# Second softmax product moved between V's first tiles, and the score products in another order

## The chip, the cores and the metric

The kernel runs on one core of one Trainium2 chip. The core has five engines with queues of their own: TensorE (PE in the profile, with its weight loads listed as PEld), VectorE (DVE), ScalarE (ACT), GpSimd (POOL) and SyncE (SP, which here only issues DMAs). The metric is the device time of one launch in microseconds, as the median of several runs.

## The reference

For each of 16 batches there are 100 rows of hidden states `x` (640 wide) and a context of 722 rows (384 wide), of which the first 718 (`enc`) are keys and values and the last 4 (`ca`) are tokens. With 8 heads of 80:

```
query = x @ Wq ; keyt = enc @ Wk ; valt = enc @ Wv
hs = mha(query, keyt, valt)                  # 100 queries, 718 keys
ca_q1 = einsum('btc,th->bch', ca, Wq_ca)[:, indices]
ca_hs1 = mha(ca_q1, x, x)                    # 100 queries, 100 keys
ca_hs2 = mha(ca_hs1 @ Wq, ca @ Wk_ca, ca @ Wv_ca)   # 4 keys
out = (hs + ca_hs2) @ Wout + b_out + x
```

`mha` scales the scores by 80 to the power -0.5, takes a softmax over the keys and multiplies by the values. All is float32.

## The kernel before

Everything is one loop over the 16 batches; each engine's instructions run in the order in which the program issues them, and the order was written out by hand. Waits between engines are semaphores that follow from tiles: an instruction that writes a buffer waits until the last reader of what was in it is done.

**The products of a batch.** The 718 keys stand in six chunks of up to 120 (`KC`), two to a group, so three key groups g = 0, 1, 2. The scores of a group (`scores`, matmuls at L688) come in two kinds. The *heads* hold 64 of the 80 columns of each head: weights of 64 rows by 64 or 56 columns, four such tiles of the array side by side. The *others* hold the remaining 16 columns of all heads: weights of 32 rows by 120 columns, again four side by side. Each float32 product is two matmul records in the profile, so the heads of a group are 64 records and the others 16. Heads and others add up in the same banks. I write H0, H1, H2 and O0, O1, O2 for them. Before, the order is H0, O0, O1, H1, H2, O2.

Scores leave PSUM by ScalarE's copies into `st` (L719 for group 1, one for each of four banks, L725 for groups 0 and 2, one for each of two pairs of banks). VectorE takes a running maximum over the three groups (`most`: L1449, then `larger`, L1440), a chain of transposes and reductions (`Maximum`, L760 to L790) spreads it, and later the maximum is subtracted and exponentiated (L1428, L1436). At the end of the batch `r_ps` (L1579) and `a_ps` (L1597) are the products with V; ScalarE copies `a_ps` out into `hsT` (L1110, `keep`).

**The tokens' attention** (`Second`) runs one batch ahead in parts. `products` writes `y_ps` for the next batch (L836), `copy` copies it to `y` (ScalarE, L857), and `softmax2` multiplies the exponentials `e1` of the present batch with `y` into `z_ps` (L898, 64 small matmuls of 32 or 4 columns) and divides on VectorE (L907, L909). Since `y` has one buffer, `copy` for the next batch must follow `softmax2` of this one. `scores2` and `softmax3` go on with the quotient `z`.

**V and K.** `Values` makes V of this batch and `Keys` makes K of the next from sums of blocks, following lists of 15 products each (`V_PLAN`, `K_PLAN`). A product goes to one of the banks A to E; after each product the bank is copied (ScalarE) or added (VectorE) to its places (`Blocks.go`, L416 and L418). `vv.go(n)` and `kk.go(n)` issue n products; `both(n)` issues n of V, then n of K. The first three products of either list go to A, B and D. A V product is four records of 320 columns over the full array, a K product four of 240.

**PSUM.** It has eight banks: two pairs (`ps2`), two of `psk` and two of `ps1`. Groups 0 and 2 of the scores take both pairs, group 1 the four single banks. `v_psA` and `v_psB` take the pairs behind group 2 (the first V product, A, waits for the first of group 2's two copies, the second, B, for the second copy). `k_psA` and `k_psB` take `psk`. `r_ps`, `a_ps`, `z_ps`, `y_ps`, the two halves of `v_psD` and `k_psD` take turns on the two `ps1` banks: the fourth bank of group 1 is the one of `a_ps`, and `k_psD` takes the bank of the first half of `v_psD`.

The order before, from the first score on:

```
st.append(scores(b, 0, tiles)); ...; st.append(scores(b, 1, tiles)); larger(1)
st.append(scores(b, 2, tiles))
now.softmax2(); second.products(); second.copy()
seen = larger(2); ...; top.go(3); both(3)
now.scores2(); top.go(1); both(2); ...
```

Of the kernel before, what the change touches and what calls it, by code (L numbers as in the profile page):

```python
# [19 lines left out]
HC = H // P  # L20
# [127 lines left out]
def kernel(  # L148
# [41 lines left out]
    def pair(name):  # L190
        tile = ps2.tile([P, 2, 512], F32, tag="ps2", name=name)
        return tile
# [21 lines left out]
    def scores_tile(name):  # L214
        return main.tile([P, 2, ROWS], F32, tag="st", name=name, bufs=NP)
# [183 lines left out]
    class Blocks:  # L399


        def __init__(self, plan):
            self.opened, self.begun = {}, set()
            self.plan = iter(enumerate(plan))
            self.ends = {bank: k for k, (bank, _, _) in enumerate(plan)}
# [264 lines left out]
        )  # L670


    def scores(b, g, tiles):

        qp, qz = tiles
        name = f"s_ps_{b}_{g}"
        if g == 1:
            s_ps = [f(f"{name}_{r}") for r, f in enumerate((psumk, psumk, psum1, psum1))]
        else:
            pairs = [pair(f"{name}_{i}") for i in range(2)]  # L680
            s_ps = [pairs[r // 2][:, r % 2] for r in range(RG)]
        n = KN
        opened = set()

        def product(a, c, rows, keys, bank, lo, rhs, last):
            u, j = KC[2 * g + a]
            first = [k for k in (0, 64) if keys.start <= k < keys.stop and (bank, k) not in opened]
            nc.tensor.matmul(  # L688
                s_ps[bank][keys, 256 * a + lo : 256 * a + lo + rhs.shape[-1]],
                kT[rows, c, u, j * KN + keys.start : j * KN + keys.stop],  # L690
                rhs,
                start=bool(first),
                stop=last,
                skip_group_check=True,
            )
            opened.update((bank, k) for k in first)

        def heads(last):
            for a in range(2):
                for c in range(HC - 1):  # L700
                    for e in range(2):
                        at = 4 * e + c
                        rows = slice(64 * e, 64 * e + 64)
                        rhs = qp[rows, c // 2, c % 2, (b % 2) * S : (b % 2 + 1) * S]
                        for keys in (slice(0, 64), slice(64, n)):
                            product(a, c, rows, keys, at // 2, at % 2 * S, rhs, last)

        def others(last):
            for a in range(2):
                for r in range(RG):  # L710
                    rows = slice(32 * r, 32 * r + 32)
                    product(a, HC - 1, rows, slice(0, n), r, 0, qz[rows, 0, b % 2], last)

        for k, part in enumerate((others, heads) if g == 1 else (heads, others)):
            part(k == 1)
        st = scores_tile(f"st_{b}_{g}")[:n]
        if g == 1:
            for r in range(RG):
                nc.scalar.copy(  # L719
                    st[:, :, 2 * r * S : 2 * (r + 1) * S],  # L720
                    s_ps[r][:n].rearrange("p (a q) -> p a q", a=2)[:, :, : 2 * S],
                )
        else:
            for i in range(2):
                nc.scalar.copy(  # L725
                    st[:, :, 4 * i * S : 4 * (i + 1) * S].rearrange(
                        "p a (r q) -> p r a q", r=2
                    ),
                    pairs[i][:n].rearrange("p r (a q) -> p r a q", a=2)[:, :, :, : 2 * S],
                )  # L730
        return st

    def wait_for(ins, other):

# [80 lines left out]
    class Second:  # L815
# [77 lines left out]
        def softmax2(self):  # L893
            b = self.b
            z_ps = (psum1 if b + 1 < B else psumk)(f"z_ps_{b}")
            for h in range(NH):
                for lo, hi in QZ:
                    nc.tensor.matmul(  # L898
                        z_ps[lo:hi, h * (HT + 1) : (h + 1) * (HT + 1)],
                        e1[:S, h * S + lo : h * S + hi],  # L900
                        self.y[:, h, :],
                        start=True,
                        stop=True,
                    )
            z_v = z_ps[:S, : NH * (HT + 1)].rearrange("p (h k) -> p h k", h=NH)
            rz = small.tile([S, NH], F32, tag="rz", name=f"rz_{b}")
            nc.vector.reciprocal(rz.unsqueeze(2), z_v[:, :, HT:])  # L907
            z = small.tile([S, NH, HT], F32, tag="z", name=f"z_{b}")
            nc.vector.tensor_tensor(  # L909
                z, z_v[:, :, :HT], rz.unsqueeze(2).to_broadcast([S, NH, HT]), ALU.mult  # L910
            )
            self.z = z
# [497 lines left out]
    for b in range(B):  # L1410
# [27 lines left out]
        def larger(i):  # L1438
            for u in range(2):
                most_now = nc.vector.tensor_tensor(  # L1440
                    most[:KN], most[:KN], st[i][:, u], ALU.max
                )
            return most_now

        st.append(scores(b, 0, tiles))
        waiting = late
        if late:
            now.exponentials1()
        nc.vector.tensor_tensor(most[:KN], st[0][:, 0], st[0][:, 1], ALU.max)  # L1449
        st.append(scores(b, 1, tiles))  # L1450
        larger(1)
        if b == 0:
            now.exponentials1()
        st.append(scores(b, 2, tiles))

        vv = Values(b, e_in, V_PLAN if b + 1 < B else END_PLAN)
        if b + 1 < B:
            kk = Keys(b + 1, enc)
        now.softmax2()
        if b + 1 < B:  # L1460
            second.products()
            second.copy()
        seen = larger(2)
        top = Maximum(most, f"{b}", True)

        if b + 1 < B:

            def both(n):
                vv.go(n)
                kk.go(n)  # L1470

            if waiting:
                wait_for(enc_sums(enc, LATE_SUMS), seen)
            if waiting:
                second.scores1(tokens=range(T - 1))
            else:
                second.scores1(seen)
            store(seen)
            if last:
                last.load(seen)  # L1480
            if b == B - 2:
                again()
            if b + 2 < B:
                m_next = load_m(b + 2, seen)
            if b == 1:
                load_outputs(nc.sync.dma_start, wout_sb, wout)
            top.go(3)
            both(3)
            now.scores2()
            top.go(1)  # L1490
            both(2)
            top.go()
            both(2)
            now.softmax3()
            if waiting:
                second.scores1(tokens=range(T - 1, T))
            if b + 2 < B:
                keys(m_next)
            both(1)
            now.spread2()  # L1500
            vv.go(2)
            kk.go(1)
            subtract(0)
            exponential(0)
            vv.go(1)
            less = subtract(1)
            if last:
                last.place(less)
                if last.b in PAIRED:
                    last.row_sums()  # L1510
                last.add_bias()
            if b == B - 2:
                mine.load(seen)
            now.values2()
            if b == B - 2:
                mine.add_bias()
            vv.go(1)
            kk.go(2)
            exponential(1)
            vv.go(1)  # L1520
            kk.go(2)
            both(1)
            both(1)
            if b == 1:
                nc.gpsimd.dma_start(out=bias, in_=bout[0].partition_broadcast(P))
            second_next, enc_next = loads()
            subtract(2)
            exponential(2)
            last_keys(b + 1, enc, b in (6, 7))
            if b + 2 < B:  # L1530
                enc_next = load_rest(b + 2, enc_next)
        else:
            last.place()
            mine.load(seen)
            top.go(3)
            vv.go(3)
            top.go(1)
            now.scores2()
            last.project_few(len(OC) - 2)
            last.project((0,), True, put=False)  # L1540
            top.go()
            now.softmax3()
            vv.go(1)
            now.spread2()
            vv.go(1)
            less = subtract(0)
            exponential(0)
            wait_for(subtract(2, nc.gpsimd), less)
            subtract(1, nc.gpsimd)
            mine.add_bias()  # L1550
            now.values2()
            vv.go(5)
            exponential(2)
            vv.go(1)
            exponential(1)
            vv.go(4)
            last.put()
# [109 lines left out]
```

## Time and profile before

| | us |
|---|---|
| median of 3 runs | 914.13 (914.01 to 916.65) |
| profiled execution, its device time | 915.1 |
| its span, first to last instruction | 913.4 |
| busy: PE, DVE, POOL, ACT | 907.1, 668.5, 619.4, 375.2 |

In the profile a row of the timeline gives start, length from the first start to the last end, engine, line, operation, tile out and in, shape and count, and in brackets the engine's idle time before it with what ended that. Matmuls overlap, so the time from the start of one row to the start of the next tells how long PE was taken. A row of a group gives busy time and the mean of one in ns, then the engine's idle time before these instructions. The granted TensorE clock is 1.0 in the whole span.

### The profile page before, as it was taken

What the parts mean: (1) busy time and instruction counts of PE and PEld (TensorE: products, weight loads), DVE (VectorE), ACT (ScalarE), POOL (GpSimd) and SP (SyncE); (2) the same over time, 40 slices, a digit from 0 to 9 for tenths busy, and PEclk for the clock granted to TensorE, in tenths of its full rate; (3) what the DMA queues carried; (4) which work ended last, traced back from release to release, by engine and by line L of the source; (5) the groups of instructions that cost most, each with busy time, mean ns of one, the idle gap of its engine ahead of it and who ended that gap; (6) DMA issues with size and microseconds to landing.
All of it is one profiled execution on the core that took longest, in us unless ns stands there. A gap on an engine that the chain in (4) does not pass through costs nothing.

```text
span 913.4 us, 26025 instructions
## 1 busy us (share of the span) xinstructions
PE 907.1 (99%) x11127; PEld 758.2 (83%) x11127; DVE 668.5 (73%) x1121; ACT 375.2 (41%) x649; POOL 619.4 (68%) x653
## 2 busy tenths in 40 slices
PE   9999999999999999999999999999999999999998
PEld 7988889787887879878788888988888888887865
DVE  4899795979649796676957769588782888828773
ACT  1354534444334453443434434344541445424451
POOL 9664786677847788476674756755796567955635
PEclk9999999999999999999999999999999999999999
DMA  8604351141302303140221402304140151401313
GB/s 275 231 13 134 61 126 37 25 124 40 103 12 71 107 21 95 44 133 12 69 76 44 133 12 70 82 7 135 43 111 11 35 140 37 111 11 45 86 34 83
DMA packets 68060, 69.48 MB, mean 76 GB/s; under 512 B 25193, under 2 KB 61353, under 8 KB 67945
## 3 DMA queue, kind: packets, MB, share of 16 engines
q1 hardware_dynamic: 67016, 66.97, 27.1%
q8 instruction: 87, 1.43, 0.7%
q10 hardware_dynamic: 464, 0.52, 0.2%
q0 software_dynamic: 464, 0.34, 0.2%
q14 instruction: 29, 0.23, 0.1%
HBM read 62.14 MB, written 8.94 MB: 78 GB/s over the span
## 4 chain that ended last, share of the span: by engine, by line
PE 98%; POOL 1%; ACT 0%; DVE 0%; issue 0%; DVEq 0%; POOLq 0%
PE s_ps L688 12%; PE v_psA L445 11%; PE v_psB L445 9%; PE k_psA L476 8%; PE a_ps L1597 7%; PE q_ps L550 7%; PE k_psB L476 7%; PE kT_ps L601 5%; PE r_ps L1579 4%; PE v_psC L445 4%; PE kT_ps L576 3%; PE k_psC L476 3%; PE y_ps L836 2%; PE v_psD L445 2%; PE v_psE L445 2%; PE o_psy L1165 2%
## 5 line engine op out<-in xcount | busy, mean ns | idle before, releaser
L871 POOL TENSOR_TENSOR e<-ca,g 100x800 f32<-100x800 f32 x60 | 91.7, 1539 | 96.9 <-DVE most L1440 74.5
L445 PE MATMUL v_psA<-wv_sb,enc 128*120 128x320 f32 x384 | 119.5, 434 | 0.0
L513 POOL TENSOR_TENSOR enc<-enc 128x240 f32<-128x240 f32 x144 | 110.0, 773 | 8.0
L445 PE MATMUL v_psB<-wv_sb,enc 128*120 128x320 f32 x320 | 99.2, 432 | 0.0
L878 POOL TENSOR_TENSOR e<-e,e 100x800 f32<-100x800 f32 x45 | 92.2, 2048 | 3.5
L445 PEld LDWEIGHTS v_psA<-wv_sb,enc 128*120 128x120 f32 x384 | 69.0, 183 | 24.7 <-DVE vs L416 0.9
L1428 DVE TENSOR_TENSOR st<-st,over 120x1600 f32<-120x1600 f32 x46 | 88.7, 1929 | 0.0
L476 PE MATMUL k_psA<-enc,wk_sb 128*128 128x240 f32 x360 | 87.6, 366 | 0.0
L476 PEld LDWEIGHTS k_psA<-enc,wk_sb 128*128 128x128 f32 x360 | 68.4, 190 | 17.1
L445 PEld LDWEIGHTS v_psB<-wv_sb,enc 128*120 128x120 f32 x320 | 58.6, 183 | 23.4
L1436 ACT ACTIVATE st<-st 120x1600 f32<-120x1600 f32 x48 | 73.9, 1539 | 8.0 <-DVE st L1428 5.5
L1440 DVE TENSOR_TENSOR most<-most,st 120x800 f32<-120x800 f32 x64 | 63.5, 993 | 16.3 <-ACT st L719 15.1
L688 PE MATMUL s_ps<-qp,kT 64*56 64x100 f32 (+1 forms) x3072 | 73.5, 248 | 0.1
L476 PE MATMUL k_psB<-enc,wk_sb 128*128 128x240 f32 x300 | 73.0, 366 | 0.0
L688 PEld LDWEIGHTS s_ps<-qp,kT 64*64 64x64 f32 (+1 forms) x3072 | 67.0, 130 | 6.1 <-issue 4.2
L1449 DVE TENSOR_TENSOR most<-st 120x800 f32<-120x800 f32 x16 | 17.4, 1090 | 73.8 <-ACT st L725 73.8
L1597 PE MATMUL a_ps<-st,vs 120*64 120x100 f32 (+1 forms) x1536 | 69.5, 250 | 0.0
L550 PE MATMUL q_ps<-xT,wq_sb 128*128 128x200 f32 x400 | 69.1, 332 | 0.0
L1597 PEld LDWEIGHTS a_ps<-st,vs 120*64 120x64 f32 (+1 forms) x1536 | 66.4, 137 | 2.7 <-issue 2.7
L550 PEld LDWEIGHTS q_ps<-xT,wq_sb 128*128 128x128 f32 x400 | 68.0, 190 | 0.2
L418 ACT COPY vs<-v_psA 120x640 f32<-120x640 f32 x48 | 33.2, 692 | 83.7 <-PE v_psA L445 83.7
L725 ACT COPY st<-s_ps 120x800 f32<-120x800 f32 x64 | 49.7, 829 | 43.2 <-PE s_ps L688 43.1
(187 smaller groups left out, 1874.7 us busy)
## 6 DMA issues: line engine op xcount, KB each, us to landing
pb<-p_d SPq DMA_DIRECT2D x32, 400.0 KB
enc<-in_enct SPq DMA_DIRECT2D x30, 240.0 KB
enc<-in_enct SPq DMA_DIRECT2D x15, 360.0 KB
xT<-in_xt SPq DMA_DIRECT2D x8, 500.0 KB
rest<-in_enct SPq DMA_DIRECT2D x31, 120.0 KB
xn<-in_x SPq DMA_DIRECT2D x11, 320.0 KB
wide_d<-p_d SPq DMA_DIRECT2D x16, 200.0 KB
pb<-wide_d SPq DMA_DIRECT2D x16, 200.0 KB
```

The costliest lines, as they stand in the source:

```text
L445: nc.tensor.matmul(at[0][j][:KN, : H // 2], a_form(self.enc, f)[:, j * KN : (j + 1) * KN], wv_sb[:, W_AT[f]], start=first, stop=last, skip ...
L476: nc.tensor.matmul(at[:, i * KT : (i + 1) * KT], wk_sb[:, W_AT[f], i], a_form(self.enc, f), start=(first and i == 0), stop=last, skip_grou ...
L513: first = nc.gpsimd.tensor_tensor(out, left, right, op)
L550: nc.tensor.matmul(q_ps[:, : 2 * S].rearrange("p (j s) -> p j s", j=2), wq_sb[:, c, n * P : (n + 1) * P], xT[:, :, c, :], start=(c == 0), ...
L688: nc.tensor.matmul(s_ps[bank][keys, 256 * a + lo : 256 * a + lo + rhs.shape[-1]], kT[rows, c, u, j * KN + keys.start : j * KN + keys.stop] ...
L725: nc.scalar.copy(st[:, :, 4 * i * S : 4 * (i + 1) * S].rearrange("p a (r q) -> p r a q", r=2), pairs[i][:n].rearrange("p r (a q) -> p r a ...
L871: first = engine.tensor_tensor(to, self.ca[:, t, :].unsqueeze(1).to_broadcast([S, NH, S]), g[:, :, t].unsqueeze(2).to_broadcast([S, NH, S] ...
L878: engine.tensor_tensor(e, e, to, ALU.add)
L1428: return engine.tensor_tensor(st[i], st[i], top.over[:KN].unsqueeze(1).to_broadcast([KN, 2, ROWS]), ALU.subtract,)
L1436: nc.scalar.activation(st[i], st[i], AF.Exp, scale=SCALE)
L1440: most_now = nc.vector.tensor_tensor(most[:KN], most[:KN], st[i][:, u], ALU.max)
L1597: nc.tensor.matmul(wides[64 * e : 64 * e + 64, h // 2], slot(i, h, FIRST[e], 64), st[i // 2][: KEYS[i], i % 2, PLACE[h] * S : (PLACE[h] + ...
```

## The change

`scores` becomes a class whose three steps (`others`, `heads`, `copy`) are issued apart. The order of the products is now O0, O1, H0, (copy of group 0), H1, (copy of group 1), H2, O2, (copy of group 2). The copy of group 0 gives its second pair of banks to VectorE, in all batches but the first. `softmax2` is cut in two: the products, and `divide2` with VectorE's reciprocal and multiplication. In batches 0 to 14 the next batch's `y_ps` products come directly behind O2, then V's tiles A and B, then the `z_ps` products, then ScalarE's copy of `y`. Behind the first step of `Maximum` stands `divide2`, then two more steps of `Maximum`, and then K's tiles A and B, V's tile D and K's tile D, where V's three tiles were followed by K's three. In batch 15, which has no next batch, the products and `divide2` stay together and follow O2.

```diff
-    def scores(b, g, tiles):
+    class Scores:
...
+        def copy(self, engines):
+            st = scores_tile(f"st_{self.b}_{self.g}")[:KN]
...
             for i in range(2):
-                nc.scalar.copy(
+                engines[i](
...
-            z_v = z_ps[:S, : NH * (HT + 1)].rearrange("p (h k) -> p h k", h=NH)
+            self.z_ps = z_ps
+
+        def divide2(self):
+            b = self.b
+            z_v = self.z_ps[:S, : NH * (HT + 1)].rearrange("p (h k) -> p h k", h=NH)
...
-        st.append(scores(b, 0, tiles))
+        by_scalar = [nc.scalar.copy] * 2
+        groups = [Scores(b, g, tiles) for g in range(2)]
+        for group in groups:
+            group.others()
+        groups[0].heads(True)
+        st.append(groups[0].copy([nc.scalar.copy, nc.vector.tensor_copy] if b else by_scalar))
         waiting = late
         if late:
             now.exponentials1()
         nc.vector.tensor_tensor(most[:KN], st[0][:, 0], st[0][:, 1], ALU.max)
-        st.append(scores(b, 1, tiles))
+        groups[1].heads(True)
+        st.append(groups[1].copy(by_scalar))
         larger(1)
         if b == 0:
             now.exponentials1()
-        st.append(scores(b, 2, tiles))
+        groups.append(Scores(b, 2, tiles))
+        groups[2].heads()
+        groups[2].others(True)
+        st.append(groups[2].copy(by_scalar))
...
-        now.softmax2()
         if b + 1 < B:
             second.products()
+            vv.go(2)
+            now.softmax2()
             second.copy()
+        else:
+            now.softmax2()
+            now.divide2()
         seen = larger(2)
...
-            top.go(3)
-            both(3)
+            top.go(1)
+            now.divide2()
+            top.go(2)
+            kk.go(2)
+            vv.go(1)
+            kk.go(1)
             now.scores2()
```

More of the change, by code (lines that the diff above doesn't have):

```diff
@@ L670, in last_keys, with __init__, product @@
         )
-    def scores(b, g, tiles):
[L675 to L687, printed above, removed]
+    class Scores:
+        def __init__(self, b, g, tiles):
+            self.b, self.g, self.tiles = b, g, tiles
+            name = f"s_ps_{b}_{g}"
+            if g == 1:
+                self.banks = [
+                    f(f"{name}_{r}") for r, f in enumerate((psumk, psumk, psum1, psum1))
+                ]
+            else:
+                self.pairs = [pair(f"{name}_{i}") for i in range(2)]
+                self.banks = [self.pairs[r // 2][:, r % 2] for r in range(RG)]
+            self.opened = set()
+        def product(self, a, c, rows, keys, bank, lo, rhs, last):
+            u, j = KC[2 * self.g + a]
+            first = [
+                k
+                for k in (0, 64)
+                if keys.start <= k < keys.stop and (bank, k) not in self.opened
+            ]
             nc.tensor.matmul(
-                s_ps[bank][keys, 256 * a + lo : 256 * a + lo + rhs.shape[-1]],
+                self.banks[bank][keys, 256 * a + lo : 256 * a + lo + rhs.shape[-1]],
                 kT[rows, c, u, j * KN + keys.start : j * KN + keys.stop],
@@ L695, in product, with heads @@
             )
-            opened.update((bank, k) for k in first)
-        def heads(last):
+            self.opened.update((bank, k) for k in first)
+        def heads(self, last=False):
+            qp, at = self.tiles[0], self.b % 2 * S
             for a in range(2):
@@ L701, in heads, with others @@
                     for e in range(2):
-                        at = 4 * e + c
+                        k = 4 * e + c
                         rows = slice(64 * e, 64 * e + 64)
[L704 to L708, printed above, removed]
+                        rhs = qp[rows, c // 2, c % 2, at : at + S]
+                        for keys in (slice(0, 64), slice(64, KN)):
+                            self.product(a, c, rows, keys, k // 2, k % 2 * S, rhs, last)
+        def others(self, last=False):
+            qz = self.tiles[1]
             for a in range(2):
@@ L711, in others @@
                     rows = slice(32 * r, 32 * r + 32)
[L712 to L723, printed above, removed]
+                    self.product(
+                        a, HC - 1, rows, slice(0, KN), r, 0, qz[rows, 0, self.b % 2], last
+                    )
+        def copy(self, engines):
+            st = scores_tile(f"st_{self.b}_{self.g}")[:KN]
+            if self.g == 1:
+                for r in range(RG):
+                    engines[r % 2](
+                        st[:, :, 2 * r * S : 2 * (r + 1) * S],
+                        self.banks[r][:KN].rearrange("p (a q) -> p a q", a=2)[
+                            :, :, : 2 * S
+                        ],
+                    )
+                return st
             for i in range(2):
-                nc.scalar.copy(
+                engines[i](
                     st[:, :, 4 * i * S : 4 * (i + 1) * S].rearrange(
@@ L728, in scores @@
                     ),
-                    pairs[i][:n].rearrange("p r (a q) -> p r a q", a=2)[:, :, :, : 2 * S],
+                    self.pairs[i][:KN].rearrange("p r (a q) -> p r a q", a=2)[
+                        :, :, :, : 2 * S
+                    ],
                 )
-        return st
+            return st
     def wait_for(ins, other):
@@ L1458 @@
             kk = Keys(b + 1, enc)
-        now.softmax2()
         if b + 1 < B:
             second.products()
+            vv.go(2)
+            now.softmax2()
             second.copy()
+        else:
+            now.softmax2()
+            now.divide2()
         seen = larger(2)
```

## The prediction

> **What bounds the kernel now.** I read the page first: the busy shares, then the chain that ended last.
>
> ```profile
> PE 907.1 (99%) x11127; PEld 758.2 (83%) x11127; DVE 668.5 (73%) x1121; ACT 375.2 (41%) x649; POOL 619.4 (68%) x653
> PE 98%; POOL 1%; ACT 0%; DVE 0%; issue 0%; DVEq 0%; POOLq 0%
> ```
>
> TensorE (PE) is busy 907.1 of 913.4 us and carries 98% of the chain. So no other engine's saving counts by itself; what counts is how many instructions PE issues (the change keeps every one), how they are ordered, and whether PE must wait. I therefore read PE's timeline at the head of one batch (batch 7), start to start, because matmuls overlap:
>
> ```profile
> 423.41 0.34 PE L1597 MATMUL a_ps<-st,vs 120*64 120x100 f32 x4
> 423.69 1.60 PE L688 MATMUL s_ps<-qp,kT 64*64 64x100 f32 x64
> 425.21 1.63 PE L688 MATMUL s_ps<-qz,kT 32*120 32x200 f32 x32
> 426.77 2.97 PE L688 MATMUL s_ps<-qp,kT 64*64 64x100 f32 x128
> 429.67 0.95 PE L688 MATMUL s_ps<-qz,kT 32*120 32x200 f32 x16
> 430.56 0.75 PE L898 MATMUL z_ps<-y,e 100*32 100x33 f32 x64
> 431.23 1.21 PE L836 MATMUL y_ps<-m,xT 128*100 128x96 f32 x10
> 432.27 1.26 PE L445 MATMUL v_psA<-wv_sb,enc 128*120 128x320 f32 x4
> 433.38 1.24 PE L445 MATMUL v_psB<-wv_sb,enc 128*120 128x320 f32 x4
> 434.45 1.24 PE L445 MATMUL v_psD<-wv_sb,enc 128*120 128x320 f32 x4
> 435.53 0.97 PE L476 MATMUL k_psA<-enc,wk_sb 128*128 128x240 f32 x4
> 436.34 0.97 PE L476 MATMUL k_psB<-enc,wk_sb 128*128 128x240 f32 x4
> ```
>
> No row has a releaser behind it: PE runs through. Call the heads' products H (64 rows per group), the others' O (16 per group). Before: H0 1.52, O0 and O1 1.56, H1 and H2 2.90, O2 0.89, z 0.67, y 1.04, then V's and K's tiles: 8.58 us to v_psA.
>
> **The change, part by part** (times from a batch's first score product; 15 batches have a next batch, batch 15 has none).
>
> *Order of the scores.* After: O0 O1, H0 H1 H2, O2. The heads run once instead of twice. Two runs of 64 would take 2 x 1.52 = 3.04, one of 128 takes 2.90: a run boundary of the heads costs 0.14, so -0.14 in each batch. O keeps two runs.
>
> *z in the middle of full-array tiles.* Between O2 and V's tiles one switch of shape goes, but z now cuts v_psB from k_psA, which adds one way out of full-array products and one way back into them. The way out is shown where kT meets r, the way back where v follows z in batch 15:
>
> ```profile
> 86.62 0.57 PE L601 MATMUL kT_ps<-rest,wk 128*128 128x240 f32 x2
> 87.03 1.78 PE L601 MATMUL kT_ps<-enc,wk 128*128 128x240 f32 x8
> 88.65 0.57 PE L601 MATMUL kT_ps<-rest,wk 128*128 128x240 f32 x2
> 89.15 2.27 PE L1579 MATMUL r_ps<-st,vs 120*32 120x100 f32 x96
> 871.89 1.34 PE L445 MATMUL v_psD<-wv_sb,enc 128*120 128x320 f32 x4
> 873.06 1.24 PE L445 MATMUL v_psA<-wv_sb,enc 128*120 128x320 f32 x4
> ```
>
> Two kT products take 0.41 before kT and 0.50 before r: 0.09 out. v_psD took 1.17 to the next start behind z, v_psB of batch 7 1.07: 0.10 back. Switches in sum: -0.14 + 0.09 + 0.10 = +0.05 a batch (ends: -0.14 if the two are free, +0.10). The Trainium skill, "TensorEngine Tiling (Array Packing)", Key Properties, says that changing the tiling mode drains the array; every boundary here agrees with about 0.1. Counting changes by that page, a batch has as many as before, and its sum would be 0.05 a batch less than mine.
>
> *What O1 in front meets.* O1's fourth bank (psum1) is the one that a_ps has just filled; ScalarE's copies of a_ps (keep) free it. Before, H0 stood between as well.
>
> ```profile
> 423.80 0.56 ACT L1110 COPY hsT<-a_ps 128x160 f32<-128x160 f32 x2 [3.02 <-PE a_ps L1597]
> 426.25 1.55 ACT L725 COPY st<-s_ps 120x800 f32<-120x800 f32 x2 [1.90 <-PE s_ps L688]
> 428.12 1.68 ACT L719 COPY st<-s_ps 120x400 f32<-120x400 f32 x4 [0.32 <-PE s_ps L688]
> 430.71 1.55 ACT L725 COPY st<-s_ps 120x800 f32<-120x800 f32 x2 [0.91 <-PE s_ps L688]
> 893.17 1.54 ACT L1436 ACTIVATE st<-st 120x1600 f32<-120x1600 f32 x1 [2.01 <-POOL st L1428]
> 894.76 0.55 PE L1579 MATMUL r_ps<-st,vs 120*32 120x100 f32 x16 [0.24 <-ACT st L1436]
> L688 PEld LDWEIGHTS s_ps<-qz,kT 32*120 32x120 f32 x768 | 31.2, 177 | 4.0
> ```
>
> The copies end at 424.36, 0.67 in; PE sees an ACT end 0.05 later (894.71 to 894.76), so 0.72. O0's 16 products take 0.67 without their boundaries (1.56 - 0.89), plus half of the 0.22 that a boundary costs: O1 would stream at 0.78, with weights (0.177) from about 0.61. About +0.1 a batch, behind which all of PE's queue stands (ends 0 and 0.15).
>
> *H2 and the copies of group 0.* H2 reuses group 0's two pairs of banks. H0 ends at 1.56 + 1.60 = 3.16. Without a boundary 64 products take 2.90 - 1.52 = 1.38, so the three take 1.52 + 2 x 1.38 = 4.28, and H2 begins 1.38 and about 0.1 of emptying before their end: 1.56 + 4.28 - 1.48 = 4.36, its weights 0.08 ahead of it at 4.28. ScalarE alone would free the second pair at 3.2 + 1.55 + 0.05 = 4.80, 0.5 late. With VectorE on that pair:
>
> ```profile
> L1449 DVE TENSOR_TENSOR most<-st 120x800 f32<-120x800 f32 x16 | 17.4, 1090 | 73.8 <-ACT st L725 73.8
> L787 DVE COPY spread<-mx 128x800 f32<-128x800 f32 x16 | 15.8, 985 | 0.5
> L1362 DVE COPY m<-m_ps 128x512 f32<-128x512 f32 x4 | 2.8, 691 | 1.1 <-PE m_ps L1354 1.1
> ```
>
> VectorE idles before its first maximum, which waits for ScalarE's two copies (to 4.1 in): 73.8 us over 15 batches, 4.9 each. So it can start at 3.2. 800 elements took it 0.985 from SBUF and 512 from PSUM 0.691; I take 0.99: free at 4.24, 0.04 to spare, cost 0 (ends 0 and 0.1). Batch 0 leaves both copies on ScalarE and pays the 0.5. The Trainium skill, same page, PSUM Bottleneck, asks for both engines on PSUM's evacuation; here that buys no time, it only pays what the new order would cost: by ScalarE alone the sum would be 14 x 0.5 higher.
>
> *v_psA without z in front.* v_psA takes the bank pair of group 2's first copy. Copies start 0.15 behind O2 (430.56 to 430.71), one takes 0.83 (row below), +0.05: 1.03 behind O2. y takes 1.04, but v_psA's weights start 0.08 ahead of it (row below), at 0.96: +0.08 (ends 0 and 0.12). Before, z's 0.67 covered it. v_psB waits for the second copy, 0.72 later, and has 1.08.
>
> ```profile
> 432.19 0.56 PEld L445 LDWEIGHTS v_psA<-wv_sb,enc 128*120 128x120 f32 x3
> 447.39 1.24 PE L445 MATMUL v_psC<-wv_sb,enc 128*120 128x320 f32 x4
> 448.13 0.96 ACT L418 COPY vs<-v_psC 120x320 f32<-120x320 f32 x2 [6.31 <-PE v_psC L445]
> L725 ACT COPY st<-s_ps 120x800 f32<-120x800 f32 x64 | 49.7, 829 | 43.2 <-PE s_ps L688 43.1
> L418 ACT COPY vs<-v_psD 120x320 f32<-120x320 f32 x32 | 13.7, 429 | 0.9
> ```
>
> *K's D tile right behind V's D tile.* V's tile D takes both psum1 banks, and K's tile D the first of them again, once ScalarE has copied it out. Before, k_psA and k_psB (1.62 us) stood between; after, the order is k_psA, k_psB, v_psD, k_psD. A first half's copy starts 0.74 behind such a tile's start (447.39 to 448.13), takes 0.43, is seen at 1.22. k_psD would start at 1.08. It starts 0.14 late, and its weights are no longer loaded under the product before, which costs the 0.10 of a refill: +0.24 (ends 0.14 and 0.30). This is the largest term; k_psD's wait holds everything of PE behind it.
>
> *Costed at nothing.* y's place, the later z, and z's quotient: v_psD's second bank is z's, freed by VectorE's quotient, now behind the third maximum and a transpose.
>
> ```profile
> 429.84 2.02 DVE L1440 TENSOR_TENSOR most<-most,st 120x800 f32<-120x800 f32 x2 [0.94 <-ACT st L719]
> 432.01 0.42 DVE L909 TENSOR_TENSOR z<-z_ps,rz 100x256 f32<-100x256 f32 x1
> 434.69 1.01 DVE L760 STREAM_TRANSPOSE turned<-most 128x800 f32<-128x800 f32 x1
> ```
>
> The third maximum can start with group 2's copies at 8.5 and takes 2.0, the transpose 1.0, reciprocal and product 0.65: done at 12.15. PE needs the bank after y (7.8), two V tiles, z and switches (3.0), two K tiles (1.62) and half a tile: about 13.0. So 0.8 of cover; if it is gone, each 0.1 costs 0.1 a batch. POOL's and SP's queues keep their order; ScalarE's copy of y moves behind two copies of V, with 1 us before v_psD needs its bank.
>
> *Sum.* Batches 1 to 14: 0.05 + 0.10 + 0.08 + 0.24 = 0.47, x 14 = 6.6. Batch 0 has no a_ps in front but ScalarE's two copies: 0.37 + 0.5 = 0.9. Batch 15 has neither K nor z inside V: -0.14 + 0.1, about 0. Together +7.5 us: span 913.4 to 920.9, profiled execution 915.1 to 922.6. The median of the runs shown, 914.13, is 1 us under that execution; on it 921.6.
>
> **The rivals.**
> - *The waits are hidden after all.* Against it: each is worked out from rows, but 0.08 and 0.1 are of the size of the rounding. If only k_psD's is hidden, 7.5 - 15 x 0.24 = +3.9, 918.0; if all are, 15 x 0.05 and little else, 914.9.
> - *Faster: the run boundary saved decides.* Place: between O1 and H1; price -0.14 x 16 = -2.2; it decides if the waits of a batch together stay under 0.14 and z's two switches are free. One PE stall in z in front could go too:
>
> ```profile
> 374.11 0.39 PE L898 MATMUL z_ps<-y,e 100*32 100x33 f32 x23 [0.36 <-issue]
> ```
>
>   Its 0.36 goes too if PE, slower issuing ahead of z, has its instructions ready. Then 914.1 - 2.2 - 0.4 = 911.5. For it: no wait shows on PE now. Against it: k_psD alone has more than 0.14.
> - *Slower still: VectorE comes late.* If its copy of group 0 (0.04 to spare) ends 0.3 late, H2 waits in each of 14 batches: +4.2, 925.8; it decides nothing below 0.1. For it: VectorE gets 14 more us of copies. Against it: it is idle there.
>
> **How the numbers follow.** My forecast, 918.5 to 924.5: 0.70. Waits hidden: 0.13, of it 0.08 near 914.9 and 0.05 near 918.0. Faster 0.06. VectorE late 0.11. The bound terms alone span 15 x (0.14 - 0.14 + 0 + 0) + 0.5, next to nothing, to 15 x (0.10 + 0.15 + 0.12 + 0.30 + 0.1) + 0.5 = 12. The range 916.5 to 926.0 leaves out the faster case, the hidden ones near 914.9 and the tail of the last. About 0.3%, 2.7 us, can be told from no change: faster 0.06, same 0.11, slower 0.83.
>
> **What would show it.** Right: k_psD starts about 1.2 us behind v_psD's start, with ScalarE's copy of v_psD as what it waited for; v_psA starts 1.1 behind y's start; O0 and O1 take 1.65; H0 to H2 take 4.28 in one run, 4.8 in batch 0. A batch's period grows by 0.4 to 0.5. Wrong: k_psD at 1.08 behind v_psD, or a period unchanged, would take the forecast away; H2 waiting for VectorE's copy would show the slower rival.

## The result and the profile after

| | before | after |
|---|---|---|
| median, us | 914.51 (914.01 to 916.65, 6 runs) | 923.22 (920.82 to 923.69, 6 runs) |
| ratio, 95% interval | | 1.008, 1.0067 to 1.0094 |
| profiled execution, its span | 915.1, 913.4 | 923.69, 922.0 |
| first score product of batch 0 to that of batch 15 | 816.21 | 823.61 |

The kernel became 8.7 us slower by the medians (0.8% by the ratio, 7.3 us); 921.6 was forecast, with a range of 916.5 to 926.0. In the profiled pair 7.40 us of it lie between the first score products of batch 0 and batch 15, and 1.25 ahead of batch 0's (48.13 before, 49.38 after).

The page of the changed kernel, busy shares and chain of work, in the form shown of before:

```profile
PE 913.4 (99%) x11127; PEld 757.1 (82%) x11127; DVE 687.8 (75%) x1136; ACT 366.0 (40%) x634; POOL 633.6 (69%) x653
PE 97%; POOL 1%; DMA 1%; DVE 0%; ACT 0%; issue 0%; SPq 0%; DVEq 0%; POOLq 0%
```

TensorE issues the same 11127 matmuls and carries the chain as before. VectorE has 19 us more, ScalarE 9 less; most of that is the moved copy, 15 times 0.99 on VectorE for 0.83 on ScalarE. So the time must be in the spacing of TensorE's instructions. The timeline of batch 7, one in which TensorE stalls nowhere else (I call such a batch undisturbed), on TensorE (start, length, then the work):

```profile
429.37 1.66 PE L696 MATMUL s_ps<-qz,kT 32*120 32x200 f32 x32
430.96 4.34 PE L696 MATMUL s_ps<-qp,kT 64*64 64x100 f32 x192
435.23 0.95 PE L696 MATMUL s_ps<-qz,kT 32*120 32x200 f32 x16
436.12 1.21 PE L851 MATMUL y_ps<-m,xT 128*100 128x96 f32 x10
437.16 1.33 PE L445 MATMUL v_psA<-wv_sb,enc 128*120 128x320 f32 x4
438.33 1.24 PE L445 MATMUL v_psB<-wv_sb,enc 128*120 128x320 f32 x4
439.50 0.75 PE L913 MATMUL z_ps<-y,e 100*32 100x33 f32 x64
440.18 1.08 PE L476 MATMUL k_psA<-enc,wk_sb 128*128 128x240 f32 x4
441.09 0.97 PE L476 MATMUL k_psB<-enc,wk_sb 128*128 128x240 f32 x4
441.90 1.24 PE L445 MATMUL v_psD<-wv_sb,enc 128*120 128x320 f32 x4
443.12 1.08 PE L476 MATMUL k_psD<-enc,wk_sb 128*128 128x240 f32 x4
444.03 1.24 PE L445 MATMUL v_psA<-wv_sb,enc 128*120 128x320 f32 x4
```

Read start to start: `k_psD` begins 1.22 behind `v_psD` (443.12 - 441.90) and holds TensorE for 0.91, where a K product in a row takes 0.81. `v_psA` and `v_psB` take 2.34 together (437.16 to 439.50), before 2.18. The heads take 4.28 in one run (430.96 to 435.23), where H0 and H1 with H2 took 1.53 + 2.90 = 4.43 before. The period, to the first score of batch 8, is 55.96, before 55.57: +0.39.

ScalarE and VectorE around it, and the groups of waits of the whole launch (last columns: us in total, times, longest):

```profile
429.49 0.55 ACT L1129 COPY hsT<-a_ps 128x160 f32<-128x160 f32 x2 [3.03 <-PE a_ps L1633]
442.64 0.96 ACT L418 COPY vs<-v_psD 120x320 f32<-120x320 f32 x2
```

```profile
432.66 0.99 DVE L738 COPY st<-s_ps 120x800 f32<-120x800 f32 x1 [5.26 <-PE s_ps L696]
441.05 0.42 DVE L928 TENSOR_TENSOR z<-z_ps,rz 100x256 f32<-100x256 f32 x1
```

```profile
PEld k_psD L476 <- ACT vs L418: 7.4, 15, 0.5
PEld s_ps L696 <- issue: 5.5, 20, 0.8
```

The second of these as the kernel before has it:

```profile
PEld s_ps L688 <- issue: 4.2, 17, 0.3
```

The first of the waits is the forecast's largest term, in each of the 15 batches that have a next one: the weight load of `k_psD` idles 0.5 (7.4 / 15) until ScalarE's copy of `v_psD` is done, and 0.24 of that reaches the products. The second are weight loads of the score products that wait for nothing that the profile shows. Most of them are no news: 16 times about 0.25 at the start of the heads' long run stand in both kernels. The rest, up to 0.8 us each, was not in the forecast's sum. Batch 6 has the longest:

```profile
371.33 1.66 PE L696 MATMUL s_ps<-qz,kT 32*120 32x200 f32 x32
372.92 2.97 PE L696 MATMUL s_ps<-qp,kT 64*64 64x100 f32 x127
376.45 1.66 PE L696 MATMUL s_ps<-qp,kT 64*56 64x100 f32 x65 [0.56 <-issue]
378.04 0.95 PE L696 MATMUL s_ps<-qz,kT 32*120 32x200 f32 x16
```

The heads take 5.12 here instead of 4.28. I call such an interruption a *hole*. After, the heads' run is longer than 4.28 in batches 2, 3, 5, 6, 8, 9, 10 and 11, by 2.6 us together. Before, there were three holes, 1.2 us: 0.54 in z (batch 6), 0.21 in y (batch 8), 0.44 in the heads (batch 11).

Summed by kind of product over batches 0 to 14, after minus before: V and K +7.6 (+0.51 in an undisturbed batch), heads +0.4 (-0.15 in each undisturbed batch, +0.39 in batch 0, the rest holes), others +0.3, z and y -0.8 (the holes of before). This is the 7.4 within the rounding.

### The profile page after: what moved, and what is told of

It is laid out like the page before. It is cut to its first block, busy times and chain, and to the rows that moved or that the text cites. A ratio compares the mean times of both kernels' runs of the same rounds, so it can differ in the third digit from the quotient of the medians.

```text
span 922.0 us, 26022 instructions
## 1 busy us (share of the span) xinstructions
PE 913.4 (99%) x11127; PEld 757.1 (82%) x11127; DVE 687.8 (75%) x1136; ACT 366.0 (40%) x634; POOL 633.6 (69%) x653
## 3 DMA queue, kind: packets, MB, share of 16 engines
q8 instruction: 87, 1.43, 0.7%
## 4 chain that ended last, share of the span: by engine, by line
PE 97%; POOL 1%; DMA 1%; DVE 0%; ACT 0%; issue 0%; SPq 0%; DVEq 0%; POOLq 0%
PE s_ps L696 12%; PE v_psA L445 11%; PE v_psB L445 9%; PE k_psA L476 8%; PE a_ps L1633 7%; PE q_ps L550 7%; PE k_psB L476 7%; PE kT_ps L601 5%; PE r_ps L1615 4%; PE v_psC L445 4%; PE kT_ps L576 3%; PE k_psC L476 3%; PE y_ps L851 2%; PE v_psD L445 2%; PE o_psy L1184 2%; PE v_psE L445 2%
## 5 line engine op out<-in xcount | busy, mean ns | idle before, releaser
L513 POOL TENSOR_TENSOR enc<-enc 128x240 f32<-128x240 f32 x144 | 112.2, 788 | 8.0
L696 PE MATMUL s_ps<-qp,kT 64*64 64x100 f32 (+1 forms) x3072 | 71.5, 247 | 1.2 <-issue 0.9
L997 POOL TENSOR_TENSOR hs<-hs,pb 128x500 f32<-128x500 f32 x48 | 63.6, 1326 | 3.8
L476 PEld LDWEIGHTS k_psB<-enc,wk_sb 128*128 128x128 f32 x300 | 57.0, 190 | 10.1
```

What stands on the lines that cost most here:

```text
L476: nc.tensor.matmul(at[:, i * KT : (i + 1) * KT], wk_sb[:, W_AT[f], i], a_form(self.enc, f), start=(first and i == 0), stop=last, skip_grou ...
L513: first = nc.gpsimd.tensor_tensor(out, left, right, op)
L696: nc.tensor.matmul(self.banks[bank][keys, 256 * a + lo : 256 * a + lo + rhs.shape[-1]], kT[rows, c, u, j * KN + keys.start : j * KN + keys ...
L997: nc.gpsimd.tensor_tensor(self.hs2, self.hs2, to, ALU.add)
```

## The experiments

All kernels here compute the whole result. Theory: the forecast's waits (`k_psD` on its bank, `v_psA` on its bank, z's two switches) make the loss, and VectorE's copy keeps H2 on time. Rivals: a single term is responsible, or the holes are, or the copy is useless. The medians stand against the kernel before in the same rounds (914.4 to 914.6).

### K's tile D later

V's next tile between V's D and K's D:

```diff
             kk.go(2)
-            vv.go(1)
+            vv.go(2)
             kk.go(1)
             now.scores2()
             top.go(1)
-            both(2)
+            vv.go(1)
+            kk.go(2)
```

> The changed kernel with one thing moved: V's next tile A stands between V's tile D and K's tile D, so that ScalarE's copy of v_psD has 1.08 us more to free the bank. Theory of the waits (K's tile D behind V's tile D costs 0.14 us of waiting and 0.10 us of an unhidden weight load in each of 15 batches): 15 x 0.24 = 3.6 us less than the changed kernel's 923.2, so 919.6; k_psD shows no wait for ScalarE. Rival (the loss lies in the long run of the heads and in the copies of the scores, and k_psD's wait would only be replaced by another one, at v_psA's or v_psE's bank): no change, 923.

Measured: 918.13, ratio 1.0044 (1.003 to 1.0057). TensorE's timeline of batch 7:

```profile
436.95 1.24 PE L445 MATMUL v_psD<-wv_sb,enc 128*120 128x320 f32 x4
438.03 1.24 PE L445 MATMUL v_psA<-wv_sb,enc 128*120 128x320 f32 x4
439.10 0.97 PE L476 MATMUL k_psD<-enc,wk_sb 128*128 128x240 f32 x4
439.91 1.24 PE L445 MATMUL v_psB<-wv_sb,enc 128*120 128x320 f32 x4
```

`v_psD` now takes 1.08 to the next start and `k_psD` 0.81: wait and refill are gone together. V's and K's products behind z take 26.25 to 26.31 instead of 26.50, 0.19 to 0.25 a batch, some 3.3 us; the median fell by 5.1, with fewer holes beside (five of them in the heads) and batch 0 beginning 2.3 us earlier in the profiled execution. The term is shown, its size by the trace and not by the median.

### The scores alone

The new order of the scores and VectorE's half copy; z, V and K as before:

```diff
+            now.softmax2()
+            now.divide2()
             second.products()
-            vv.go(2)
-            now.softmax2()
             second.copy()
...
-            top.go(1)
-            now.divide2()
-            top.go(2)
-            kk.go(2)
-            vv.go(1)
-            kk.go(1)
+            top.go(3)
+            both(3)
```

> The new order of the scores and VectorE's half of the copies alone; the second softmax product, V's and K's tiles stand as before. Theory of the waits: one run boundary less in each of 16 batches (16 x -0.14 = -2.2), O1's wait for a_ps 0.03 as the changed kernel shows it (+0.4), batch 0's copies +0.5: 1.3 less than before, 913.2. Rival (the long run of heads makes TensorE wait for its own instructions, as the 0.2 to 0.8 us holes without a releaser in H0 to H2 of the changed kernel suggest, about 1.5 us more of them than before): 914.5 to 915, no gain.

Measured: 914.48, ratio 1.0007 (0.9998 to 1.0017). The rival was right: the 0.15 saved in each batch is in the trace (4.28 wherever nothing interrupts), but the heads' run is longer in batches 2 to 6, 8, 10, 11 and 13, by 3.9 us in sum, and z in batch 6 by 0.73. Batch 4 on TensorE:

```profile
262.77 1.66 PE L696 MATMUL s_ps<-qz,kT 32*120 32x200 f32 x32
264.36 4.34 PE L696 MATMUL s_ps<-qp,kT 64*64 64x100 f32 x190
269.20 0.33 PE L696 MATMUL s_ps<-qp,kT 64*56 64x100 f32 x2 [0.50 <-issue]
269.46 0.95 PE L696 MATMUL s_ps<-qz,kT 32*120 32x200 f32 x16
```

So the score part of the change gained nothing. In the median it cost nothing either; in the profiled execution batch 0 to batch 15 takes 818.02, 1.8 more than before, while batch 0 begins 1.0 earlier. The greater part of the loss lies in z's place and what follows it.

### z alone

z behind V's A and B and the changed order of K and V, with scores and copies of before:

```diff
-        groups = [Scores(b, g, tiles) for g in range(2)]
-        for group in groups:
-            group.others()
-        groups[0].heads(True)
-        st.append(groups[0].copy([nc.scalar.copy, nc.vector.tensor_copy] if b else by_scalar))
+        groups = [Scores(b, 0, tiles)]
+        groups[0].heads()
+        groups[0].others(True)
+        st.append(groups[0].copy(by_scalar))
```

> The second softmax product behind V's tiles A and B, with the K and V tiles in the changed order, alone; the scores in the order of before, all copies by ScalarE. Theory of the waits: 15 x (0.19 for one more way out of and back into the full array + 0.08 for v_psA + 0.24 for k_psD) = 7.7 more than before, 922.2; few holes in the heads' runs. Rival (most of the loss is in the scores' part): 916 to 918.

Measured: 920.88, ratio 1.0072 (1.0059 to 1.0084). No hole in any batch: H0 1.53, O0 and O1 1.56, H1 and H2 2.90, O2 0.88, z 0.68, each batch the same. Each of the batches 1 to 14 is 0.51 longer, but for 6, 8 and 11, where the holes of before are gone; batch 0, which had other waits before, is 0.15 longer. The rows that carry it are those of the change:

```profile
437.68 1.24 PE L445 MATMUL v_psD<-wv_sb,enc 128*120 128x320 f32 x4
438.89 1.08 PE L476 MATMUL k_psD<-enc,wk_sb 128*128 128x240 f32 x4
439.81 1.24 PE L445 MATMUL v_psA<-wv_sb,enc 128*120 128x320 f32 x4
```

Summed over the 15 batches V and K take 7.5 more, nearly the 7.6 of the full change. With `k_psD`'s 0.24 and `v_psA`'s 0.07 taken off, 0.20 of the 0.51 are left for the way out of the full-array products into z and back, where the forecast had 0.09 + 0.10. That agrees with the Trainium skill, "TensorEngine Tiling (Array Packing)", Key Properties, which says that a change of the tiling mode drains the array; it gives no price for it.

### Both copies by ScalarE

```diff
-        st.append(groups[0].copy([nc.scalar.copy, nc.vector.tensor_copy] if b else by_scalar))
+        st.append(groups[0].copy(by_scalar))
```

> The changed kernel with both copies of group 0 on ScalarE in all batches. Theory of the waits: H2 then waits 0.5 us for its second pair of banks in each of batches 1 to 14 as it does in batch 0, +7.5 with batch 15: 930.7, and H0 to H2 take 4.8 instead of 4.3. Rival (VectorE's copy hides nothing, H2's holes come from instruction supply): 923.

Measured: 926.99, ratio 1.0142 (1.0129 to 1.0156), halfway between the two. The heads take 4.81 to 4.82 in every batch, +0.54, as the theory says; batch 7:

```profile
431.67 3.13 PE L696 MATMUL s_ps<-qp,kT 64*64 64x100 f32 x132
434.97 1.58 PE L696 MATMUL s_ps<-qp,kT 64*64 64x100 f32 x60 [0.17 <-ACT st L738]
```

But there is no hole beside that wait in any batch: from batch 0's first score to batch 15's it takes 828.74, 5.1 more than the changed kernel and not 14 x 0.54 = 7.6, and the 2.5 that fail are about the 2.7 of holes. A pause in the middle of the run takes the holes away: the first sign that they come from the run's length.

### The others of group 2 in between

The scores alone, with a shorter heads' run (O0 O1 H0 H1 O2 H2):

```diff
-        groups[2].heads()
-        groups[2].others(True)
+        groups[2].others()
+        groups[2].heads(True)
```

> The new order of the scores and VectorE's half copy alone, but with the others' products of group 2 moved between the heads' of group 1 and of group 2, so that the heads' run is 128 records long, as in the kernel before, and not 192; one more switch (0.14) in each of 16 batches. If the holes come from the length of the run: H128 shows 2.86 in most batches, the holes fall from 3.4 us to about the 1.2 us that the kernel before has, and the time stays at 914.5 (914.5 + 16 x 0.14 - 3.4 + 1.2). Rival, holes that come anywhere whatever the run's length: about 3.4 us of them stay, in H128 or H64, and the time is 916.7.

Measured: 915.86, ratio 1.0009 (0.9998 to 1.002), between the two expectations in time; the trace decides. Batch 4, the one shown above:

```profile
265.51 2.97 PE L696 MATMUL s_ps<-qp,kT 64*64 64x100 f32 x128
268.41 0.95 PE L696 MATMUL s_ps<-qz,kT 32*120 32x200 f32 x16
269.29 1.60 PE L696 MATMUL s_ps<-qp,kT 64*64 64x100 f32 x64
```

2.90 in 15 of 16 batches and 3.19 in batch 6, where z has 0.31 more too: 0.6 us of holes instead of 4.7 (3.9 in the heads, 0.73 in z of batch 6). Batch 0 to batch 15 takes 815.91, 0.3 less than before, so the score part costs nothing within the batches once the holes are gone; the rest lies at the ends (the last batch's `a_ps` took 5.28 in this execution instead of 4.28).

### z alone with K's tile D later

```diff
             kk.go(2)
-            vv.go(1)
+            vv.go(2)
             kk.go(1)
             now.scores2()
             top.go(1)
-            both(2)
+            vv.go(1)
+            kk.go(2)
```

> The second softmax product behind V's first tiles alone (scores and copies of the kernel before), with V's next tile between V's and K's tile on the shared bank. By the theory of the waits the bank's wait goes (0.20 to 0.24 in each of 15 batches) and what is left against the kernel before is V's start behind y and the switches of the second softmax product, 0.28 in each of 15 batches: 920.9 - 3.3 = 917.6. Rival, the bank's wait was not what the place of the product costs: 920 or more.

Measured: 918.2, ratio 1.004 (1.0026 to 1.0054). The undisturbed period is 0.27 to 0.32 over before: z's switches and `v_psA`, 0.28 by the expectation. `k_psD` begins without a wait, as in the first experiment. The fall from 920.88 is 2.7, with 0.4 us of holes that were not there.

### Batch 0 in the old order

The kernel with O2 in between, with H0, O0, O1 in batch 0:

```diff
-        for group in groups:
-            group.others()
-        groups[0].heads(True)
+        if b:
+            for group in groups:
+                group.others()
+            groups[0].heads(True)
+        else:
+            groups[0].heads()
+            groups[0].others(True)
+            groups[1].others()
```

> As the kernel with the others' products of group 2 in between, and in batch 0 the score groups in the order of the kernel before, so that the heads of group 2 don't wait there for ScalarE's second copy. Theory: 0.5 us less than that kernel (914.0 if it takes 914.5), and the heads of group 1 and 2 of batch 0 without a wait. Rival, something else in batch 0 ends last: the same time as that kernel.

Measured: 915.11, ratio 1.0006 (0.9997 to 1.0016), 0.75 under that kernel and no difference from before that can be told. In batch 0 group 2 no longer waits for ScalarE's copy: H1 has 1.53 and O2 0.88 (1.27 in that kernel). Yet batch 0 as a whole takes 47.51 against 47.53, as the rival had it: a weight load of K's tile E then idles 0.3 until VectorE has added a block. The 0.75 between the medians is therefore not shown to come from batch 0. The kernel isn't better than the one before the change: as many switches, and holes of 0.36 (heads) and 0.85 (z) in batch 6 and 0.47 (y) in batch 8.

### Where the holes come from

The profile counts what each DMA queue moved (packets, MB, share of the engines). The row of the changed kernel, and the same of before:

```profile
q8 instruction: 87, 1.43, 0.7%
```

1.43 MB over TensorE's 11127 matmuls and 11127 weight loads are 64 bytes for each, and 87 transfers make 16 KB, 256 instructions, apiece. The trace records them, 1.1 us long on average; with the 128 instructions inserted below it has 88. Outside batch 0, the ten traces of this case that have holes show 55 of over about 0.13 us, and each of them ends 1.2 to 1.6 us behind the end of the last such transfer, though one comes only every 10 us. Numbered in TensorE's stream, six holes of the changed kernel end at 3738, 5008, 7806, 9078, 11876 and 14674: steps of 5, 11, 5, 11 and 11 times 254, within 4. A heads' run issues 384 instructions in 4.28 us, so 256 of them last 2.84, while O0 and O1 need 1.56 for 64. This suggests that a hole comes where a whole transfer falls into the run. To move only the position in the stream, 128 instructions were put at the start of the launch:

```diff
     for _ in range(7):
-        nc.tensor.matmul(idle_ps[:, :P], idle, idle, start=True, stop=True)
+        nc.tensor.matmul(idle_ps[:, :64], idle, idle[:, :64], start=True, stop=True)
+    for _ in range(32):
+        nc.tensor.matmul(idle_ps[:32, :16], idle[:, :32], idle[:, :16], start=True, stop=True)
```

> The new order of the scores and VectorE's half copy alone, with 32 small matmuls (64 records, each with its weight load: 128 instructions) more at the very start of the launch, where TensorE waits for its first data anyway; the seven matmuls that stood there are half as wide. Nothing else changes, but every later instruction of TensorE stands 128 places further in its stream. Theory of the instruction transfers: the stream comes in transfers of 16 KB, which the counts make 256 instructions, and a hole comes where a whole one of them falls into the heads' run. The places of the holes then move by half a transfer: holes in batches 1, 7, 9, 12, 14 and 15, which had none, and none in batches 2, 3, 8, 10 and 11, which had them; the holes in sum some 2 us more, 916.5. Rival, holes that come from the stage of the kernel (data transfers at that time, the engines' work beside it): the same batches as without the insertion, and 914.5.

And 256 instructions, with 16 columns for the seven and 64 small ones:

> As the half-block kernel, but with 64 small matmuls (256 instructions, one whole transfer) and the seven others narrower still. Theory of the instruction transfers: the places of the holes are where they were without the insertion, H192 longer than 4.28 in batches 2 to 6, 8, 10, 11 and 13, and the time is 914.5 again. Rival, that the insertion itself costs: as much or more than the half-block kernel. Rival, holes by the stage: the same batches here too, but then also in the half-block kernel.

The inserted products weren't free, as a rival of the last expectation had it: the 64 records took 3.5 us and the 128 took 6.9 at the start, where the heads' rate of 22 ns a record would give 1.4 and 2.8, so that batch 0 begins at 51.70 and 55.06 instead of 47.09 and the medians are 922.17 and 923.56. The times therefore decide nothing, but the places do. Length of the heads' run above 4.28, in us, in the batches named:

| kernel | batches 2, 3, 8, 10, 11 | batches 1, 9, 14, 15 | batches 4, 5, 6, 13 |
|---|---|---|---|
| scores alone | 0.15, 0.42, 0.50, 0.40, 0.35 | 0, 0, 0, 0 | 0.82, 0.58, 0.32, 0.39 |
| 128 instructions more | 0, 0, 0, 0, 0 | 0.13, 0.13, 0.42, 0.49 | 0.73, 0.44, 0.77, 0.61 |
| 256 instructions more | 0.27, 0.10, 0.47, 0.15, 0.14 | 0, 0, 0, 0 | 0.09, 0.65, 0.28, 0.43 |

Half a transfer further, the five batches that were to lose their holes lost them, and of the six that were to get one four did; in 7 and 12 it came in z instead (1.22 and 1.07 for 0.68). Batches 4, 5, 6 and 13 kept theirs: by the count a whole transfer begins within 20 instructions of the run's start in 4, 5 and 13 after the shift, and inside it in 6; the expectation had not named them. A whole transfer further, the same nine batches as without the insertion have them. Two rows show it, batch 2 with 128 more and with 256 more:

```profile
156.39 4.34 PE L696 MATMUL s_ps<-qp,kT 64*64 64x100 f32 x192
```

```profile
159.59 4.62 PE L696 MATMUL s_ps<-qp,kT 64*64 64x100 f32 x192
```

The insertion of 128 instructions into the kernel before:

> The kernel before with the same insertion of 128 instructions. Theory of the instruction transfers: the few holes of the kernel before (batch 6 in z, batch 8 in y, batch 11 in H128, 1.2 us) go from there and others come, at most in some heads' runs of 128 that begin near the start of a transfer; estimated from the time that 254 matmuls and loads take at each place, 1 us more in sum, 915.5. Rival: the holes stay in z, y and H128 of batches 6, 8 and 11, and the time is 914.5.

Measured: 920.85, of which 3.8 stand ahead of batch 0 (51.92 against 48.13). The holes of before are gone from z of batch 6, y of batch 8 and the heads of batch 11; others came in z of batches 5, 7, 8, 12 and 13, for instance batch 5:

```profile
321.40 0.53 PE L898 MATMUL z_ps<-y,e 100*32 100x33 f32 x36
322.38 0.44 PE L898 MATMUL z_ps<-y,e 100*32 100x33 f32 x28 [0.45 <-issue]
```

Batch 0 to batch 15 takes 817.17, +0.96, where +1 was expected; that they come in z, whose 128 instructions take 0.68, and not in the heads, was not. The rival by stage is out: the stages were the same and the holes moved with the stream. Why a transfer that takes 1.1 us comes too late for these runs, no run shows.

## Why the prediction was right, point by point

- **`k_psD` right behind `v_psD`, +0.24 a batch:** right in size and cause. 1.22 behind, releaser ScalarE's copy, 0.14 of wait and 0.10 of refill; moved away, both are gone. With 3.6 us the largest term, as forecast.
- **z between full-array tiles, +0.09 and +0.10:** right; `v_psB` takes 1.17 ahead of z (438.33 to 439.50) for 1.08, `k_psA` 0.91 behind it (440.18 to 441.09) for 0.81, and z alone leaves 0.20 for the two. No run removed the switches by themselves.
- **`v_psA` without z in front, +0.08:** size and cause hold, the sign named doesn't. `v_psA`'s record starts 1.04 behind y and not 1.1, but its four records take 1.17 instead of 1.11. The first of group 2's copies ends at 436.27 + 0.83 = 437.10, and the weights load at 437.15, only with the matmul's start at 437.16 and not 0.08 ahead of it as before, so that the loss lies inside the product:

```profile
436.27 1.55 ACT L738 COPY st<-s_ps 120x800 f32<-120x800 f32 x2 [0.91 <-PE s_ps L696]
437.15 0.82 PEld L445 LDWEIGHTS v_psA<-wv_sb,enc 128*120 128x120 f32 x4
```

- **Heads' boundary saved, -0.14:** right where nothing interrupts (-0.15).
- **O1 waits for `a_ps`'s copies, +0.10:** mis-sized. O0 and O1 take 1.56 to 1.59, and 1.65 only in batch 15: +0.02. The step let O1's first product wait; the code goes through the banks in the order 0 to 3, and the bank of `a_ps` is the fourth, so three products come ahead of it. This is read from the code and the times; no run took it apart.
- **H2 and VectorE's copy, cost 0; batch 0 +0.5:** right. With ScalarE alone every batch shows the 0.54 that batch 0 shows here. The 0.04 to spare was enough. Batch 0 as a whole grew by 0.54 (48.03 for 47.49) where 0.9 was forecast, since 0.37 of waits that it had before, in O2, z, V and K, are gone.
- **z's quotient hidden:** right: it is done at 441.47, and `v_psD`, which takes its bank, starts at 441.90 without a wait.
- **What the sum left out:** the holes, +2.6 in the heads and -1.2 of before's. The forecast saw one such stall in front of z and gave it only to the faster rival. They nearly cancel O1's 14 x 0.08 and the 0.4 of batch 0, and so 7.5 was forecast and 7.4 found within the batches: that close a hit is luck, by errors of opposite sign.
- **The rivals.** Waits hidden: out, by `k_psD`'s releaser. Faster: z's switches aren't free, and the saving of 2.2 that it builds on goes to the holes, as the scores alone show. VectorE late: out.
- **Still open:** the 1.25 us ahead of batch 0. In the traces without an insertion the first score product comes at 46.8 to 49.4. Two things differ there. The changed kernel waits 2.2 for the first K data and starts its first kT product at 7.18, the kernel before at 5.83. And the granted clock of the changed kernel was 0.50 from 8.2 to 11.6; in the kernel before, whose page has 1.0 there, a kT product of two records took 0.80 until 9.86 (7.56 to 8.36) and 0.41 from then on (10.37 to 10.78), which points to half the clock there too. No run was made to tell what either comes from; none of the change's edits stands ahead of batch 0's scores in the program.

## What to carry to other kernels

Price a moved step on a bound engine by what it now stands beside: the two tiles that were pushed together on one bank cost more than the step itself. An order that lets the bound engine issue faster gains only as long as its instructions arrive, so count them: here runs of 384 at 90 a microsecond had holes in up to 9 of 16 batches, and runs of 256 in two at most. And a stall without a releaser that recurs at even steps of the instruction count is no accident of a run; a shift of the stream by half a step tells.

## What the runs showed of the hardware

- TensorE's instructions come in transfers of 16 KB while it runs (87, and 88 with 128 instructions more). Where 256 of them were used up in about 2.8 us, it stood still for 0.1 to 0.8 us, and the holes kept their places in the stream when other work moved. The Trainium skill, "Runtime: NRT & Kernel Launch", Instruction fetch mechanics, describes refills in blocks of 16 KiB, 256 instructions each, which these counts bear out; it also says that the fetch is hidden because the engine issues more slowly than it is filled, and here, at 90 instructions a microsecond, it was not hidden.
- A pause of 0.17 us for a semaphore in the middle of the run (0.54 with what hangs on it) left no hole in the launch, and gave back about a third of its price.
- 64 small matmul records with their loads took 3.5 us at the start of the launch, 55 ns each, where the heads' take 22. How much of that is the clock isn't shown: right behind them in that trace two kT records took 0.80 (10.36 to 11.16), and 0.40 from 13.95 on.
